# Second layer: where the spectral matrices, the keys' spectra and some element-wise products are computed

## The chip, the cores and the metric

The kernel runs on one core of one Trainium2 chip. Times are microseconds (us) on the device for one execution of the whole program; lower is better. The core has a matrix engine (PE, TensorE; its weight loads are listed as PEld), three engines for element-wise work (DVE or VectorE, ACT or ScalarE, POOL or GpSimd), and queues from which transfers (DMAs) are started; most are started on SP, some on ACT's own queue. Two on-chip memories matter here: SBUF, and PSUM, into which PE writes[...]. A kernel waits for transfers and for other engines by semaphores.

## The reference

Two layers with a residual each, on an image tensor of 4 x 48 x 48 x 128:

```python
    x = x + _L0_conv_ref(_gn(x), ...)
    x = x + _L1_conv_ref(_gn(x), ...)
```

The first is a selective scan in four directions; the change does not touch it. The second takes the image as 4 images of T = 48 channels, each 48 rows (H) by 128 columns (W), and is an attention over the channels whose keys, queries and values are made by spectral convolutions, followed by two more of these:

```python
def _spec_conv(x, w, out_hw):
    xf = jnp.fft.rfft2(x, norm='forward')
    top = jnp.einsum('bimn,iomn->bomn', xf[:, :, :m1, :m2], wc[0])
    bot = jnp.einsum('bimn,iomn->bomn', xf[:, :, -m1:, :m2], wc[1])
    of = of.at[:, :, :m1, :m2].set(top)
    of = of.at[:, :, -m1:, :m2].set(bot)
    return jnp.fft.irfft2(of, s=(Ho, Wo), norm='forward')

def _forward(x, ...):
    xa_n = _inorm(xa, norm_g[0], norm_b[0])
    k = _fno_layer(xa_n, wK, wKs, bKs, (H // 2, W // 2))
    q = _fno_layer(xa_n, wQ, wQs, bQs, (H // 2, W // 2))
    v = _fno_layer(xa_n, wV, wVs, bVs, (H, W))
    scores = jnp.einsum('bhtd,bhsd->bhts', qs, ks) / (np.sqrt(ks.shape[-1]) * TEMPERATURE)
    out = jnp.einsum('bhts,bhsd->bhtd', jax.nn.softmax(scores, axis=-1), vs)
    projd = _fno_layer(out, wP, wPs, bPs, (H, W))
    attention = _inorm(projd + xa, norm_g[1], norm_b[1])
    an = _inorm(attention, norm_g[2], norm_b[2])
    m = _fno_layer(an, wM0, wM0s, bM0s, (H, W), (norm_g[3], norm_b[3]), act=True)
    m = _fno_layer(m, wM1, wM1s, bM1s, (H, W), (norm_g[4], norm_b[4]), act=False)
    return (_inorm(m, norm_g[5], norm_b[5]) + attention).reshape(B, T, H, W)
```

There are 32 heads. `_inorm` normalises each channel's image; `_fno_layer` is a spectral convolution plus a pointwise one. All is float32.

## The kernel before

Layer 0 fills the time up to about 4215 us. Its instructions and those of the last part of layer 1 (the `Strand` class) go through `Ordered`, line 50, which keeps each engine's instructions in the order of the program; that is why so many rows of the profile name L50. The rest of layer 1, in `layer1`, is put in order for each engine by a scheduler, which may move independent instructions past each other; each engine then runs its own list in order.

Layer 1 goes through these stages (times of the profiled execution):

- 4209 to 4258: loads; copies `gblk` and statistics over groups (`bn_stats`), meanwhile the products of the weights of projection and values (`gw`) are transposed and written to DRAM as `dgt`.
- 4258 to 4311: `group_affine` (matmul `gm_l`), the affine map on `xa`, then `first_norm`: means `pm_in`, differences, variances `pv_in`, and the factor `in_r` (line 718). `prepare` loads the weights of keys and queries (`w_wQ`, `w_wK`: many small DMAs on SP, lines 893 to 899) and makes their product `g_qk` by a chain of small DVE instructions.
- 4311 to 4355: `forward_w`, a Fourier transform along the width: PE writes `pa_x`, DVE scales it into `a_x` (two buffers), six DMAs write `da_x` to DRAM, and `load_a2` reads it back turned around as `a2`. Meanwhile PE transposes `xa` into `pxn`, and ACT scales that into `xnt` with the factor `r_t` (from the small matmul `pr`).
- 4356 to 4392: `spectral_weights`, lines 951 to 979. The two MLP convolutions' weights `wM0` and `wM1` (loaded into `w2`) become, for each of 32 frequencies, a 96 x 96 matrix along the height. In 16 rounds of four frequencies POOL makes two products `wih`, PE two matmuls `psw`, ACT copies them into `spw` (one buffer), and a DMA writes that to `sp_d` in DRAM. The matrices are read (as `sp_m`) by the strands, long after.
- 4392 to 4419: `psel` picks the frequencies for queries `qs` and keys `ks` out of `a2`; `pplain` and `ps0` give the scores' part without weights.
- 4419 to 4459: the keys' spectra, in the code the last loop of this block: for each of 16 (image, group of 8 frequencies), two half spectra `pxt` on PE, two ACT copies into `xt` (two buffers), one POOL addition, one DMA to `dxt`. `dxt` is used by the next stage but one.
- 4460 to 4557: the scores. For each of two pairs of images and 12 `jn`, DVE (two of three) or POOL (the third) makes `f`, 128 x 3072, and PE multiplies it with `qs` into four banks `sc`, eight matmuls per `jn`; a last product with `d_qk`; then the softmax, transposes `pat` and copies to `attn_c`.
- 4557 to 4835: the products with the values (`v`, `v3`, `acc`).
- 4835 to 5126: two strands of 96 channels each, by turns: each has phases p0 to p5 with a tail after each (t0 to t5) that is stepped through during the other strand's phase. p1 adds the projection, p2 is the first MLP convolution's part along the height (`pe_m`, `e_m`, with the sums of squares `sqe` into `st_m`, and POOL's `m<-xa,sw`), p3 its part along the width (`pi_m`) with the GELU, p4 and p5 the same for the second convolution and the output. `total` reduces the sums (`red`, `tot_m`), and `product` makes the squares, with frequency 0 halved by the factor `first_k`. In p5, `skip` multiplies eight rows of `m` by `qm` (the tile `sw`) and adds `y` (the image `xa`), and `put` transposes (`pf`), adds a bias (`ot`) and writes the result.

The lines that start the changed parts:

```python
        r0 = first_norm(psst, work, xa)
        prepare()
        ...
        spectral_weights(psum, work)
        ...
            def skip(q):
                for i in range(2):
                    v = self.m[:, 24 * i + q : 24 * i + q + 8]
                    on.gpsimd.tensor_mul(v, v, over(self.qm, 8))
                    on.vector.tensor_add(v, v, self.y[:, 24 * i + q : 24 * i + q + 8])
```

Of the kernel before, what the change touches and what calls it, by code (L numbers as in the profile page):

```python
# [10 lines left out]
F32 = mybir.dt.float32  # L11
BF16 = mybir.dt.bfloat16
AF = mybir.ActivationFunctionType
ALU = mybir.AluOpType
# [15 lines left out]
NH = 32  # L30
# [612 lines left out]
def layer1(ctx, tc, io, x1_dram, out):  # L643
# [5 lines left out]
    nc = tc.nc  # L649
# [298 lines left out]
    def spectral_weights(psum, work):  # L948


        fht = []
        for i, m in enumerate((fh, fhi)):
            p = psum.tile([128, 512], F32, tag="mm", name=f"pfht{i}")
            nc.tensor.transpose(p[0:96, 0:96], m, ident[0:96, 0:96])
            t = work.tile([96, 96], F32, tag=f"fht{i}", name=f"fht{i}", bufs=1)
            nc.scalar.copy(t, p[0:96, 0:96])
            fht.append(t)
        none = work.tile([1, 2, 1], F32, tag="none", name="none", bufs=1)
        nc.gpsimd.memset(none, 0.0)
        for n in range(2):  # L960
            w2 = work.tile([96, 2, 32], F32, tag="w2", name=f"w2_{n}", bufs=2)
            for c in range(2):
                for i in range(2):
                    nc.sync.dma_start(w2[i * 48 : (i + 1) * 48, c], io[f"wM{n}"][c])
            for i in range(2):
                nc.sync.dma_start(w2[48 * i : 48 * i + 1, :, 0:1], none)
            for k0 in range(0, 32, 4):
                p = psum.tile([128, 512], F32, tag="mm", name=f"psw{n}_{k0}")
                for c in range(2):
                    t = work.tile([96, 4, 96], F32, tag="wih", name=f"wih{n}_{k0}_{c}")  # L970
                    nc.gpsimd.tensor_mul(
                        t,
                        ih[:, None].to_broadcast([96, 4, 96]),
                        w2[:, c, k0 : k0 + 4, None].to_broadcast([96, 4, 96]),
                    )
                    nc.tensor.matmul(p[0:96, 0:384], fht[c], t, start=(c == 0), stop=(c == 1))
                t = work.tile([96, 4, 96], F32, tag="spw", name=f"spw{n}_{k0}", bufs=1)
                nc.scalar.copy(t, p[0:96, 0:384].rearrange("p (k m) -> p k m", m=96))
                nc.sync.dma_start(sp_d[n][:, k0 : k0 + 4], t)


    with ExitStack() as ph:
        psum = ph.enter_context(tc.tile_pool(name="l1_ps0", bufs=3, space=PSUM))
        psst = ph.enter_context(tc.tile_pool(name="l1_ps0s", bufs=1, space=PSUM))
        work = ph.enter_context(tc.tile_pool(name="l1_work0", bufs=2))
        mv = small.tile([128, B, 2], F32, tag="mv", name="mv1")
        for b in range(B):
            st = small.tile([128, 6, 6], F32, tag="st", name=f"st1_{b}")
# [29 lines left out]
        for p in range(2):  # L1018
            for q in range(0, H, 4):
# [8 lines left out]
                    AF.Copy,  # L1028
                    scale=r_t[:, p : p + 1],
                )  # L1030
        spectral_weights(psum, work)

        for j in range(4):
            for dst, sel, sel0, one in ((qs, sel_q, sel_q0, one_q), (ks, sel_k, sel_k0, one_k)):
# [37 lines left out]
            nc.tensor.matmul(p[0:T, 0:T], u32[:, bs], u32[:, bs], start=False, stop=True)  # L1072
            nc.scalar.copy(s0[:, b], p[0:T, 0:T])

        for b in range(B):
            for k in range(4):
                xt = work.tile([T, 3, NC], F32, tag="xt", name=f"xt{b}_{k}")
                for e in range(2):
                    p = psum.tile([128, 512], F32, tag="mm", name=f"pxt{b}_{k}_{e}")
                    for i in range(4):  # L1080
                        nc.tensor.matmul(
                            p[0:T, i * 96 : (i + 1) * 96],
                            a2[:, 8 * k + 4 * e + i, b * T : (b + 1) * T],
                            fh,
                            start=True,
                            stop=True,
                        )
                    nc.scalar.copy(
                        xt[:, 0:2].rearrange("t c (k y) -> t k c y", y=48)[:, 4 * e : 4 * e + 4],
                        p[0:T, 0:384].rearrange("t (k c y) -> t k c y", c=2, y=48),  # L1090
                    )
                nc.gpsimd.tensor_add(xt[:, 2], xt[:, 0], xt[:, 1])
                nc.sync.dma_start(dxt[b, k], xt.rearrange("r c n -> r (c n)"))


    with ExitStack() as ph:
        p2 = ph.enter_context(tc.tile_pool(name="l1_p2", bufs=2))
        pf = ph.enter_context(tc.tile_pool(name="l1_pf", bufs=3))
        ps_1 = ph.enter_context(tc.tile_pool(name="l1_ps1", bufs=1, space=PSUM))
        pst = ph.enter_context(tc.tile_pool(name="l1_pst", bufs=2, space=PSUM))  # L1100
        gp = ps_1.tile([128, 3, 4, NH], F32, name="gp_qk")
        nc.scalar.copy(gp, g_qk)
        scale = 2.0 * math.sqrt((H // 2) * (W // 2))
        for pair in range(2):
            sc = ps_1.tile([128, 4, 512], F32, tag="sc", name=f"sc{pair}")
            for jn in range(12):
                j, n = divmod(jn, 3)
                f = pf.tile([128, 2, NH, T], F32, tag="f", name=f"f{pair}_{jn}")
                shape = [128, 2, NH, T]
                on_pool = jn % 3 == 2  # L1110
                (nc.gpsimd if on_pool else nc.vector).tensor_mul(
                    f,
                    (g_qk if on_pool else gp)[:, n, j, None, :, None].to_broadcast(shape),
                    ks[:, j, n, 2 * pair : 2 * pair + 2, None].to_broadcast(shape),
                )
                for g in range(4):
                    for b in range(2):
                        nc.tensor.matmul(
                            sc[64 * b : 64 * b + 64, g, 0 : 8 * T],
                            qs[:, j, n, 2 * pair + b],  # L1120
                            f[:, b, 8 * g : 8 * g + 8],
                            start=(jn == 0),
                            stop=False,
                        )
            for g in range(4):
                for b in range(2):
                    nc.tensor.matmul(
# [6 lines left out]
            for g in range(4):  # L1134
# [18 lines left out]
                for q in range(3):  # L1153
# [4 lines left out]
                    attn_c[:, 2 * pair : 2 * pair + 2, g],  # L1158
                    p[:, 0:384].rearrange("p (q b t) -> p b q t", b=2, t=64),
                )  # L1160
    early.close()


# [144 lines left out]
    eps2 = vec.tile([128, 1], F32, name="eps2")  # L1308
    nc.gpsimd.memset(eps2, 1e-10)
    cst = vec.tile([128, 8], F32, name="cst")  # L1310
    ga, gb, c0, cm, b15, gw0, w11 = (cst[:, i : i + 1] for i in range(7))
    nc.vector.tensor_mul(ga, n_g[:, 1:2], n_g[:, 1:2])
    nc.vector.tensor_scalar(ga, ga, 1e-5, None, ALU.add)
    nc.vector.tensor_mul(gb, n_g[:, 1:2], n_g[:, 2:3])
# [5 lines left out]
    nc.vector.tensor_scalar(cm, cm, -1.0, None, ALU.mult)  # L1320
    nc.vector.tensor_add(b15, n_b[:, 1:2], n_b[:, 5:6])
    nc.vector.tensor_mul(w11, wsm[1], wsm[1])
    a2_all = None

    class Strand:
# [91 lines left out]
        def product(self, e, other, k0, name):  # L1417
# [3 lines left out]
            else:  # L1421
                on.vector.tensor_mul(t, e, other)
            if k0 == 0:
                on.vector.tensor_scalar(t[:, 0], t[:, 0], first_k, None, ALU.mult)
            return [t[:, 4 * i : 4 * i + 4] for i in range(2)]


# [185 lines left out]
        def t4(self):  # L1613
# [10 lines left out]
            on.vector.tensor_mul(v5, t4, v4)  # L1624
            on.vector.tensor_mul(u, t4, cv)
            on.vector.tensor_mul(v5, v5, t4)
            on.vector.tensor_scalar(u, u, wsm[1], 2.0, ALU.mult, ALU.mult)
            on.vector.tensor_add(v5, v5, self.vm)
            on.vector.tensor_add(v5, v5, u)
            s5 = self.rsqrt("s5", v5, eps)  # L1630
# [24 lines left out]
        def p5(self):  # L1655


            def skip(q):
                for i in range(2):
                    v = self.m[:, 24 * i + q : 24 * i + q + 8]  # L1660
                    on.gpsimd.tensor_mul(v, v, over(self.qm, 8))
                    on.vector.tensor_add(v, v, self.y[:, 24 * i + q : 24 * i + q + 8])

            for t in range(6):
# [25 lines left out]
    def over(t, n=QB):  # L1690
        return t[:, None, :].to_broadcast([128, n, P])
# [127 lines left out]
```

## Time and profile before

| | |
|---|---|
| three runs | 5125.19, 5130.29, 5134.14 us; median 5130.29 |
| the profiled execution | 5128.24 us |
| its span | 5126.5 us |
| mean granted PE clock | 0.922 |
| busy in the span: PE, DVE, POOL, ACT | 4220.8, 4231.3, 4054.3, 2907.2 us |
| layer 1 | about 4209 to 5126.5 us |

The profile is of one execution. A row of the timeline or of a group reads: start in us, duration in us (of all its instructions when it ends in xN), engine, line, operation, output<-inputs, shapes, and in square brackets the time for which the engine had been idle before it and what ended that. Part 2 of the page cuts the span into 40 slices of 128 us and gives each engine's busy share in tenths; the last seven to eight slices are layer 1. A sum over a stretch gives, after the stretch and its length, the busy time and number of instructions of PE, PEld, DVE, ACT and POOL, then the granted clock of PE, the share of DMA and its GB/s.

In layer 0 each of DVE and POOL is busy for nearly the whole time; in layer 1 the stages follow each other with different engines busy in each.

### The profile page before, as it was taken

Reading aid. Unit: us, or ns where it says so; the run is one execution under the profiler, and the core shown is the slowest. Engines: PE = TensorE matmul, PEld = TensorE weight load, DVE = VectorE, ACT = ScalarE, POOL = GpSimd, SP = SyncE. Lnnn points to the kernel's source line nnn. Section 1 sums busy time; section 2 is a strip of 40 time slices with the busy share of each in tenths; the row PEclk is TensorE's granted clock in tenths of the full one; section 3 lists DMA queues with packets and bytes.
Section 4 is the critical chain, followed back from the end, with each engine's and each line's share of the span. In section 5 each row is a group of like instructions: output and inputs, shape, how many; then the busy total and the mean of one; then the engine's idle time right before and its main releaser. Section 6 shows DMA issues by size and latency. Waiting matters only on the chain. (4 is left out here: it accounts for less than half of the span.)

```text
span 5126.5 us, 44328 instructions
## 1 busy us (share of the span) xinstructions
PE 4220.8 (82%) x12344; PEld 1901.0 (37%) x12344; DVE 4231.3 (83%) x2887; ACT 2907.2 (57%) x6438; POOL 4054.3 (79%) x2223
## 2 busy tenths in 40 slices
PE   6889898878898988888989888878787866888876
PEld 3334333333343333333433333333333323443343
DVE  3689998989899989899999898999999964166545
ACT  3666666666565676666666766666565633213343
POOL 3589998989899988898999888899999860446433
PEclk8999999999999999999999999999999887889877
DMA  1223232323333322232333232333333226136536
GB/s 53 76 84 104 95 113 91 102 86 100 94 107 102 106 90 98 87 102 93 105 106 102 92 99 88 105 99 106 98 101 97 90 67 139 47 83 183 152 90 142
DMA packets 276767, 509.25 MB, mean 99 GB/s; under 512 B 100602, under 2 KB 185434, under 8 KB 276326
## 3 DMA queue, kind: packets, MB, share of 16 engines
q1 hardware_dynamic: 265846, 502.66, 32.1%
q10 hardware_dynamic: 10672, 3.76, 0.4%
q8 instruction: 97, 1.59, 0.1%
q14 instruction: 152, 1.25, 0.1%
HBM read 462.58 MB, written 43.72 MB: 99 GB/s over the span
## 5 line engine op out<-in xcount | busy, mean ns | idle before, releaser
L50 POOL TENSOR_TENSOR hc<-h,cbc 128x960 f32<-128x960 f32 (+1 forms) x1280 | 2716.5, 2137 | 464.7 <-DVE h L50 336.1
L50 DVE TENSOR_TENSOR_SCAN h<-da,carry,db 128x961 f32<-128x961 f32 (+1 forms) x1280 | 2701.0, 2129 | 122.1 <-ACT carry L50 87.8
L50 ACT ACTIVATE da<-dt,a_neg 128x480 f32<-128x480 f32 (+1 forms) x2560 | 1661.3, 649 | 1251.3 <-DVE h L50 1206.3
L50 PE MATMUL yp<-hc,ident 128*128 128x480 f32 (+1 forms) x5120 | 2276.5, 572 | 7.1 <-POOL hc L50 6.9
L50 PEld LDWEIGHTS yp<-hc,ident 128*128 128x128 f32 x5120 | 1007.8, 199 | 1421.9 <-issue 1011.1
L50 DVE TENSOR_TENSOR db<-du,pb 128x960 f32<-128x960 f32 (+1 forms) x960 | 1062.3, 1107 | 210.2 <-PE pb L50 154.6
L50 PE MATMUL pb<-bs,pick 112*128 112x480 bf16 (+1 forms) x960 | 361.6, 377 | 399.1 <-DVE db L50 397.2
L50 POOL TENSOR_TENSOR db<-du,bbc 128x960 f32<-128x960 f32 (+1 forms) x320 | 687.9, 2150 | 0.0
L50 PE MATMUL pc<-pad,cdiag 128*128 128x480 f32 (+1 forms) x630 | 283.3, 561 | 10.7 <-ACT pad L50 10.7
L1236 POOL TENSOR_TENSOR v<-grep,xrep 128x768 f32<-128x768 f32 x96 | 173.7, 1820 | 107.3 <-PE acc L1240 52.2
L50 POOL TENSOR_TENSOR du<-dt,xc 128x480 f32<-128x480 f32 (+1 forms) x160 | 204.3, 1277 | 37.7 <-ACT dt L50 37.7
L50 PE MATMUL px<-xc,w_xp 128*112 128x480 f32 (+1 forms) x320 | 216.2, 763 | 16.9 <-ACT xc L50 13.3
L1240 PE MATMUL acc<-v,attn_c 128*64 128x384 f32 x1152 | 211.7, 505 | 22.2 <-POOL v L1236 17.2
L50 ACT COPY db<-carry 128x1 f32<-128x1 f32 x1280 | 226.0, 177 | 7.0 <-DVE db L50 3.7
L1232 DVE TENSOR_TENSOR v<-gp,xrep 128x1536 f32<-128x1536 f32 x96 | 164.5, 1753 | 78.5 <-DMA xrep<-dxt 36.2
L50 PEld LDWEIGHTS <-pick 112*128 112x128 bf16 x960 | 97.9, 102 | 333.9 <-issue 310.3
L50 PE MATMUL pd<-xd,w_dt 8*128 8x480 f32 (+1 forms) x320 | 168.6, 607 | 39.8 <-ACT bs L50 25.5
L50 ACT ACT_TABLE_LOAD x146 | 187.3, 1283 | 23.4 <-PE gv_g L50 13.7
L50 ACT COPY carry<-h 128x2 f32<-128x2 f32 x1024 | 192.6, 188 | 0.0
L50 PEld LDWEIGHTS pc<-pad,cdiag 128*128 128x128 f32 x630 | 122.1, 195 | 144.2 <-issue 114.9
L50 PE MATMUL yp<-y,ident 128*128 128x480 f32 (+1 forms) x240 | 166.2, 822 | 0.2
L1240 PEld LDWEIGHTS acc<-v,attn_c 128*64 128x64 f32 x1152 | 90.3, 140 | 139.9 <-issue 52.6
(366 smaller groups left out, 3192.0 us busy)
## 6 DMA issues: line engine op xcount, KB each, us to landing
cbc<-cd SPq DMA_DIRECT2D x512, 480.0 KB
bbc<-cd SPq DMA_DIRECT2D x256, 240.0 KB
cbc<-cd SPq DMA_DIRECT2D x128, 384.0 KB
xrep<-dxt SPq DMA_DIRECT2D x384, 72.0 KB
grep<-dgt SPq DMA_DIRECT2D x32, 576.0 KB
bbc<-cd SPq DMA_DIRECT2D x64, 192.0 KB
dgt<-gtt SPq DMA_DIRECT2D x4, 2304.0 KB
x<-in_xT SPq DMA_DIRECT2D x16, 288.0 KB
```

What stands on the lines that cost most here:

```text
L50: return lambda *args, **kw: self._tc.keep_in_program_order(emit(*args, **kw))
L1232: nc.vector.tensor_mul(v, gp[:, None, :, 0:NC].to_broadcast([128, 2, 2, NC]), x[:, :, 0:2])
L1236: nc.gpsimd.tensor_mul(v3, r[:, 2:3].to_broadcast([128, 2, NC]), x[:, :, 2])
L1240: nc.tensor.matmul(acc[c][64 * b : 64 * b + 64, 0:NC], attn_c[:, 2 * pair + b, g, q], v[:, b, c] if c < 2 else v3[:, b], start=first, stop ...
```

## The change

Four parts, all in layer 1.

1. `spectral_weights` is called before the statistics, at the start of its block, instead of after the transposes. Its loads of `wM` (12 small DMAs) go to ACT's queue instead of SP's.
2. The keys' spectra become a generator, `keys`, whose halves are issued between the score products, one or two after each `jn`. `xt` has one buffer instead of two, and its products have one PSUM bank. `f` is made in two halves, one for each image of the pair, in five buffers of half the size instead of three.
3. The factor `first_k` of `product` and the factor `wsm[1] * 2` of t4 are applied by ACT (`self.times`, an activation with a scale) instead of DVE; the second one's value is made ahead, as `w2`.
4. `skip` multiplies on DVE instead of POOL.

```diff
@@ spectral_weights
-                    nc.sync.dma_start(w2[i * 48 : (i + 1) * 48, c], io[f"wM{n}"][c])
+                    nc.scalar.dma_start(w2[i * 48 : (i + 1) * 48, c], io[f"wM{n}"][c])
             for i in range(2):
-                nc.sync.dma_start(w2[48 * i : 48 * i + 1, :, 0:1], none)
+                nc.scalar.dma_start(w2[48 * i : 48 * i + 1, :, 0:1], none)
@@ layer1
         work = ph.enter_context(tc.tile_pool(name="l1_work0", bufs=2))
+        spectral_weights(psum, work)
         mv = small.tile([128, B, 2], F32, tag="mv", name="mv1")
...
-        spectral_weights(psum, work)
...
-        for b in range(B):
-            for k in range(4):
-                xt = work.tile([T, 3, NC], F32, tag="xt", name=f"xt{b}_{k}")
...
-        pf = ph.enter_context(tc.tile_pool(name="l1_pf", bufs=3))
+        pf = ph.enter_context(tc.tile_pool(name="l1_pf", bufs=5))
...
+        psx = ph.enter_context(tc.tile_pool(name="l1_psx", bufs=1, space=PSUM))
+        def keys():
+            for b in range(B):
+                for k in range(4):
+                    xt = p2.tile([T, 3, NC], F32, tag="xt", name=f"xt{b}_{k}", bufs=1)
+                    for e in range(2):
+                        p = psx.tile([128, 512], F32, tag="xt", name=f"pxt{b}_{k}_{e}")
+                        for i in range(4):
+                            nc.tensor.matmul(
+                                p[0:T, i * 96 : (i + 1) * 96],
+                                a2[:, 8 * k + 4 * e + i, b * T : (b + 1) * T],
+                                fh,
+                                start=True,
+                                stop=True,
+                            )
+                        nc.scalar.copy(
+                            xt[:, 0:2].rearrange("t c (k y) -> t k c y", y=48)[:, 4 * e : 4 * e + 4],
+                            p[0:T, 0:384].rearrange("t (k c y) -> t k c y", c=2, y=48),
+                        )
+                        yield
+                    nc.gpsimd.tensor_add(xt[:, 2], xt[:, 0], xt[:, 1])
+                    nc.sync.dma_start(dxt[b, k], xt.rearrange("r c n -> r (c n)"))
+        beside = keys()
...
-                f = pf.tile([128, 2, NH, T], F32, tag="f", name=f"f{pair}_{jn}")
-                shape = [128, 2, NH, T]
+                shape = [128, NH, T]
                 on_pool = jn % 3 == 2
-                (nc.gpsimd if on_pool else nc.vector).tensor_mul(
-                    f,
-                    (g_qk if on_pool else gp)[:, n, j, None, :, None].to_broadcast(shape),
-                    ks[:, j, n, 2 * pair : 2 * pair + 2, None].to_broadcast(shape),
-                )
+                f = []
+                for b in range(2):
+                    f.append(pf.tile(shape, F32, tag="f", name=f"f{pair}_{jn}_{b}"))
+                    (nc.gpsimd if on_pool else nc.vector).tensor_mul(
+                        f[b],
+                        (g_qk if on_pool else gp)[:, n, j, :, None].to_broadcast(shape),
+                        ks[:, j, n, 2 * pair + b, None].to_broadcast(shape),
+                    )
...
-                            f[:, b, 8 * g : 8 * g + 8],
+                            f[b][:, 8 * g : 8 * g + 8],
...
+                for _ in range(2 - jn % 2 if pair == 0 else 1 + jn % 2):
+                    next(beside, None)
...
+        for _ in beside:
+            pass
@@ layer1, constants
+    nc.vector.tensor_scalar(w2, wsm[1], 2.0, None, ALU.mult)
@@ Strand.product
             if k0 == 0:
-                on.vector.tensor_scalar(t[:, 0], t[:, 0], first_k, None, ALU.mult)
+                self.times(t[:, 0], t[:, 0], first_k)
@@ Strand.t4
-            on.vector.tensor_scalar(u, u, wsm[1], 2.0, ALU.mult, ALU.mult)
+            self.times(u, u, w2)
@@ Strand.p5, skip
-                    on.gpsimd.tensor_mul(v, v, over(self.qm, 8))
+                    on.vector.tensor_mul(v, v, over(self.qm, 8))
```

## The prediction

> **What bounds the kernel now.** I read the page first, then the timeline of the second layer (4209 to 5126 us of a span of 5126.5), then sums over stretches, then single tiles. The page's part 2 shows where there is anything to win: in the last eight of the 40 slices DVE and POOL fall from nine tenths to between one and six, while PE stays at seven or eight.
>
> ```profile
> PE   6889898878898988888989888878787866888876
> DVE  3689998989899989899999898999999964166545
> POOL 3589998989899988898999888899999860446433
> ```
>
> The part of the page on the chain that ended last names only 14 pieces from 5114.89 us on, so the order of stages must be read from the timeline. The sums over stretches show two stages (us, then busy time of PE, PEld, DVE, ACT, POOL) in which DVE does nothing: 4357 to 4392 makes spectral weights, 4419 to 4460 the keys' spectra.
>
> ```profile
> 4357.00:4392.00 35.00, 30.02 (x64) 9.78 (x64) 0.00 (x0) 6.53 (x16) 24.21 (x30) 0.85 0.19 55
> 4419.00:4460.00 41.00, 29.14 (x256) 26.89 (x255) 0.00 (x0) 14.57 (x34) 15.79 (x16) 0.79 0.39 87
> ```
>
> In the timeline the first one's pace is a DMA: each copy into `spw`, which has one buffer, waits for the transfer out of it. The second ends in a wait of DVE for the last transfer of a key spectrum; the line above it is the work the keys are now put beside, where PE is held by `f`.
>
> ```profile
> 4364.87 0.47 ACT L978 COPY spw<-psw 96x384 f32<-96x384 f32 x1 [1.99 <-DMA sp_d<-spw]
> ...
> 4431.62 1.52 PE L1081 MATMUL pxt<-fh,a_x 96*48 96x96 f32 x16 [0.15 <-ACT xt L1088]
> ...
> 4460.43 6.62 DVE L1111 TENSOR_TENSOR f<-gp_qk,ks 128x3072 f32<-128x3072 f32 x2 [45.33 <-DMA dxt<-xt]
> ...
> 4478.72 7.96 PE L1118 MATMUL sc<-f,qs 128*64 128x384 f32 x48 [0.41 <-POOL f L1111]
> ```
>
> Later a single multiplication of 96x96 numbers holds DVE for 26.14 us, while POOL runs 24 products without a gap; PE waits 23.84 us behind it.
>
> ```profile
> 4932.95 26.14 DVE L50 TENSOR_SCALAR sqe<-sqe,first_k 96x96 f32<-96x96 f32 x1 [6.42 <-ACT sqe L50]
> ...
> 4937.81 21.21 POOL L50 TENSOR_TENSOR xa<-xa,s 128x768 f32<-128x768 f32 x12
> 4959.01 0.54 DVE L50 TENSOR_REDUCE red<-st_m 128x96 f32<-128x384 f32 x1
> 4959.61 0.50 PEld L50 LDWEIGHTS tot_m<-red,g 128*128 128x128 f32 x2 [24.08 <-DVE red L50]
> 4959.61 0.74 PE L50 MATMUL tot_m<-red,g 128*128 128x96 f32 x2 [23.84 <-DVE red L50]
> ```
>
> And in the last stage DVE waits for POOL's products.
>
> ```profile
> 5068.92 12.77 POOL L50 TENSOR_TENSOR m<-m,sw 128x768 f32<-128x768 f32 x6
> 5070.75 5.01 DVE L50 TENSOR_TENSOR m<-m,xa 128x768 f32<-128x768 f32 x2 [10.21 <-POOL m L50]
> ```
>
> **What the Trainium skill says.** "SBUF — State Buffer", section "Who interferes with whom": a DVE instruction with two SBUF inputs, or one in a two-port performance mode, shares a port pair with a GpSimd instruction reading SBUF; the lock is held for the whole instruction; PE and ACT never wait for it. The trace agrees: `first_k` took 266 ns at best and 26142 ns at worst, and `e_m<-e_m,t` 0.95 us alone, 2.47 beside POOL. That one instruction is passed over by some fourteen POOL instructions is in the trace, not in the page. "DMA: Bandwidth & Descriptors" gives a fixed cost of about 2 us per DMA; the trace has 1.99 us of wait per `spw`.
>
> **Spectral matrices ahead.** What it would remove: `a_x` is back at 4355.5, and `psel` starts at 4392.44, so 36.9 us are spent on these matrices. But the order of PE's instructions in the new program has only two transposes and four of the 16 `psw` before the statistics; the other twelve come behind `pr`, ahead of `pa_x`, which begins the forward transform. ACT has one `spw` early, 15 behind `r_t`. With one buffer each costs 0.47 us of copy and 1.98 of wait, 2.44 in the trace. So:
> - the four early `psw` took 8.5 us (4357.1 to 4365.5) in before; `gm_l`, at 4258.7, then starts about 5 later (2 to 7: part lies in the time in which DVE stands until 4248.5);
> - 12 loads of `wM` now lie on ACT's queue in the tail of layer 0: mostly in ACT's gaps, +1 (0 to 6);
> - `in_r` came at 4311.3; the 15 copies take 15 x 2.44 = 36.6, less the PSUM buffers that let PE go ahead (3 buffers): `pa_x` can begin near 4342 and the first `a_x` be done at 4350 where it was 4313.4; the g_qk chain of DVE is behind the same loads of `w_wK` on SP, which stand between the `sp_d` transfers. The last `da_x` leaves near 4365 (was 4336.29); `pu` came 19.2 after it: `psel` at 4385.5, with the 6 from above 4391.5, against 4392.44.
> Then `psel` to `ps0` without the transfers is about 1.5 shorter. I take -1 in all for this part: the work has moved past the transform, not beside it. Bounds: -36 if `pa_x` isn't held, +12 if the delays ahead are the upper ones.
>
> **Keys between the products.** Removed: the stage from 4418.9 to 4460.3. The first `f` can start at 4417.4 + (-1 + 1) of the part above, 42.9 earlier. Added: PE gets 32 halves of 0.76 (1.52 for two), 24.3 us. The products before: `d_qk` of the first pair ends 40.6 after the first `f`, of the second 86.4; a period of 8.36 for three jn, of which 7.96 is PE. PE is thus nearly full, and the 24.3 us lie on the path, save what fits its waits (0.41 a period, and the two starts). `xt` and its PSUM bank have one buffer: a round of two halves, two copies of 0.47, one add of 0.99 behind POOL's `f` halves (2.67 each) and a transfer of about 2.2 comes to some 6 us. Following the instructions by hand I get 48.6 for the first pair and 102.2 for the second: +15.8. One more for the last `dxt`, which now stands ahead of the loads for the next stage on SP. Five half-size buffers of `f` for three whole ones change nothing: half h takes the place of h-5, near enough double buffering. -42.9 + 15.8 + 1 = -26; with the 1 above I write -25 here and -1 there (bounds -34, PE's waits taking half of it, to -12, a round of 7).
>
> **Small factors off DVE.** `first_k` on ACT costs about 0.37 (row `s<-s,n_g`; here 96x96). The 26.14 goes. `red` then starts at 4934.3, `tot_m` near 4936; `e_m` is loaded from 4936.72 on and lands near 4945; from `red` to `pi_m` the trace has 9.74 (4959.01 to 4968.75), which gives 4944; `t<-t,s` and `e_m<-e_m,t` have two SBUF inputs and POOL runs until 4959, so 2 more, as in the pairs 0.95 and 2.47. `pi_m` at 4946 against 4968.75: -22 (0 to -25). What is late next is the landing of `e_m`, one us before. The other three `first_k` and `u` on ACT: nothing, they're 0.3 to 1.7 us beside PE's work. The chain behind it (p3, p4, p5) has no other input that is later, so the gain lasts.
>
> **Last products on DVE.** POOL's six cost 12.77 and 13.57 per strand (2.13 to 2.26 each), and in strand 0 they stand behind the `xr` additions, until 5067.16, though `sw` was there at 5055.7. On DVE a round of q is `e_m` 0.95, two products and two sums of 0.93, four of 0.50: 6.7, three times 20. Strand 0's p5 ran from 5059.6 to 5094 with p4's end beside it; the 10.21 of wait goes, DVE's contended sums (5.01 and 3.42 for two, alone 1.82) too, and 5.6 of products come: -5 to -10. Strand 1: 5097.35 to 5120.65 is 23.3; 20 now: -3.5. If the cover, PE's `pf` and ACT's `ot`, isn't as short as DVE, nothing below 5097 + 18 is possible. Together -12 (-8 to -15).
>
> Sum: -1 - 25 - 22 - 12 = -60. The profiled execution took 5128.24, 1.7 over its span, and lies 2 below the median 5130.29: 5068 as a profile, 5070 as a median.
>
> **Rivals.**
> A: the matrices do get hidden, because `pa_x` overtakes or the copies don't wait in that place (their transfers overlap idle queues). For: DVE and POOL are idle there. Against: PE's order is fixed, and one buffer. 5070 - 34 = 5036.
> B: the stall moves to the next DVE instruction with two SBUF inputs (`t<-t,s`, until POOL ends at 4959.02). For: the same queue of POOL's 24. Against: DVE's tensor_tensor instructions get in by turns elsewhere (13.27 for four beside POOL at 4286.90). Then the 22 are lost: 5092.
> C, the slower side: the single `xt` buffer holds PE, which stands in order: each `pxt` waits for a transfer that waits for an add behind two `f` halves. The worst round is 1.5 + 0.9 + 5.3 + 1 + 2.2 = 10.9; 16 of these are 174 where I have 102. It ends the gain from (102 + 60)/16 = 10.1 and makes it measurably slower from 10.8; at 11.2, 5070 + (179 - 102) = 5147. Against: POOL has an `f` at only every third jn.
> D: the delays ahead of the statistics and a round of 7 both come in: +12 + 13, 5095.
>
> **How the numbers follow.** Forecast 0.5, A 0.2, B 0.15, D 0.1, C 0.05. Likeliest: 5070, its own range 5052 to 5086. The range reaches to A and to B and D: 5030 to 5106; outside is C and a joint B and D. A measurement of this kernel can tell about 0.2%, 10 us. Faster than 5120: all but C and a rest of D: 0.92; within 0.03; slower 0.05.
>
> **What would show it.** In the new profile: a `spw` row with some 2 us of DMA wait still, but between `r_t` and `pa_x`, and the first `da_x` near 4350; the first `f` near 4417 and the second pair's `d_qk` some 102 after; no DVE instruction over 6 us after 4900 and `pi_m` about 10 behind `red`; `m<-m,sw` on DVE at 0.93. I'd be wrong if `psel` starts below 4375 (A), if a small DVE instruction of 10 us or more stands there (B), or if `pxt` waits 4 us and more for `xt` (C).

## The result and the profile after

The changed kernel took 5085.36 us (median of five runs, 5073.73 to 5089.75) against 5130.29 before (median of five, 5115.78 to 5134.14): a ratio of 0.9918, with a 95% interval of 0.9899 to 0.9937. It is faster by 0.8%, where 1.2% (5070) was predicted. The profiled execution has a span of 5083.1 us, 43.4 less than before.

The busy shares by slice, for the lines shown of the kernel before:

```profile
PE   6889898888798988887989888878787785888876
DVE  3689998989899989898999898999999983356536
POOL 4589998988899989798999898899999872346531
```

Counted from 1, slice 35 of DVE, which held the idle stages, has filled from 1 to 3: the scores have moved forward into it. In the last slice DVE went from 5 to 6 and POOL from 3 to 1, the products of the last stage. The rest is read best by taking the same events in both timelines, each counted from the start of the load of `xa` (4219.7 before, 4218.1 after; 1.6 us of the gain lie in layer 0, which is the same in both, and over all traces this start lies between 4215.7 and 4221.8). Every event is given by the start of its instruction.

| event, us after the load of xa | before | after | change of the stage that ends here | predicted |
|---|---|---|---|---|
| first `psel` | 172.7 | 172.7 | 0.0 | -1 |
| first `f` | 240.7 | 193.7 | -47.0 | -43 |
| last product with `d_qk` | 326.5 | 300.7 | +21.2 | +16 |
| first `acc` | 355.1 | 329.6 | +0.3 | +1 |
| last `acc` | 611.5 | 590.4 | +4.4 | 0 |
| first `red` of `st_m` | 739.3 | 693.5 | -24.7 | -25 |
| first `pi_m` of p3 | 749.0 | 719.7 | +16.5 | +3 |
| first `ot` | 857.8 | 817.8 | -10.7 | -8 |
| last `ot` | 902.3 | 860.8 | -1.5 | -4 |

The first row says that up to `psel` nothing was gained by moving the matrices; the second and third say that the keys' stage is gone and that the scores pay nearly half of it. All this was in the sum, though not in these sizes. The row of `pi_m` was not: of the 24.7 us won up to `red`, 16.5 are lost again within the next 26. The timeline of the changed kernel shows where:

```profile
4911.57 0.56 DVE L50 TENSOR_REDUCE red<-st_m 128x96 f32<-128x384 f32 x1 [8.35 <-PE st_m L50]
...
4915.37 21.20 POOL L50 TENSOR_TENSOR xa<-xa,s 128x768 f32<-128x768 f32 x12
4915.56 0.75 DVE L50 RECIPROCAL t<-t 128x96 f32<-128x96 f32 x1 [1.81 <-ACT t L50]
...
4916.35 20.35 DVE L50 TENSOR_TENSOR t<-t,s 128x96 f32<-128x96 f32 x1
...
4936.73 0.96 DVE L50 TENSOR_TENSOR e_m<-e_m,t 128x768 f32<-128x768 f32 x1
4937.79 3.02 PE L50 MATMUL pi_m<-e_m,iw 64*128 64x384 f32 x8 [15.86 <-issue]
```

`red` runs at 4911.57, as it should with the 26.14 us gone. But the next DVE instruction with two operands in SBUF, `t<-t,s` with 96 elements a row, is recorded with 20.35 us, and it ends when POOL's twelve products end (4936.57). `RECIPROCAL`, just before it and with one operand, took its usual 0.75 beside the first of these products. The stall has not gone; it has found another instruction.

### The profile page after: what moved, and what is told of

It is laid out like the page before. It is cut to its first block, busy times and chain, and to the rows that moved or that the text cites. A ratio compares the mean times of both kernels' runs of the same rounds, so it can differ in the third digit from the quotient of the medians.

```text
span 5083.1 us, 44364 instructions
## 1 busy us (share of the span) xinstructions
PE 4214.9 (83%) x12344; PEld 1897.5 (37%) x12344; DVE 4225.4 (83%) x2908; ACT 2911.3 (57%) x6446; POOL 4033.8 (79%) x2219
## 5 line engine op out<-in xcount | busy, mean ns | idle before, releaser
L1252 PE MATMUL acc<-v,attn_c 128*64 128x384 f32 x1152 | 212.8, 511 | 25.8 <-POOL v L1248 15.8
```

Of the source, the lines that this page charges most:

```text
L1252: nc.tensor.matmul(acc[c][64 * b : 64 * b + 64, 0:NC], attn_c[:, 2 * pair + b, g, q], v[:, b, c] if c < 2 else v3[:, b], start=first, stop ...
```

## The experiments

Runs of one kernel differ: eleven of the kernel before, beside the ninth to eleventh experiment, lie between 5108.34 and 5140.23. So the experiments are read by intervals between events in their traces, and by the time of the program only where there were several runs. The stage of `acc`, which no experiment touches, took from 253.4 to 267.0 us over all traces: the 4.4 in the table is within what this stage varies by itself.

**First: `first_k` on ACT and nothing else**, in the kernel before.

```diff
-                on.vector.tensor_scalar(t[:, 0], t[:, 0], first_k, None, ALU.mult)
+                self.times(t[:, 0], t[:, 0], first_k)
```

> The kernel before with one edit: first_k is applied by ACT. Theory 1 (the obstacle is POOL's unbroken queue of 24 products; any DVE instruction with two SBUF inputs that comes while it runs is passed over until its end): the 26.14 us goes, but t<-t,s then stands until POOL ends near 4959, and pi_m comes about 8 us earlier than in the kernel before (near 4960), the whole 5120. Theory 2 (only the in-place scaling by first_k is passed over): pi_m 22 us earlier, near 4946, the whole 5106.

It took 5127.47 in one run (5120 was expected), 5135.03 the kernel before beside it.

```profile
4947.75 0.56 DVE L50 TENSOR_REDUCE red<-st_m 128x96 f32<-128x384 f32 x1 [7.86 <-PE st_m L50]
...
4951.43 21.22 POOL L50 TENSOR_TENSOR xa<-xa,s 128x768 f32<-128x768 f32 x12
...
4952.52 20.24 DVE L50 TENSOR_TENSOR t<-t,s 128x96 f32<-128x96 f32 x1
...
4973.85 3.05 PE L50 MATMUL pi_m<-e_m,iw 64*128 64x384 f32 x8 [15.75 <-issue]
```

`t<-t,s` stands for 20.24. Here the way to POOL's row was longer than in the other two traces (its first product lies 87 us behind the first `pe_p`, not 80; PE's granted clock over this stretch was 0.74, and 0.82 in the kernel before), so the start of POOL's 24 products is the fair zero: `pi_m` follows it by 52.2 in the kernel before (4916.60 to 4968.75), by 43.7 in the changed kernel (4894.11 to 4937.79) and by 43.7 here (4930.2 to 4973.85). Counted so, the edit is worth 8.4 us, as theory 1 said, and this is what used to follow the end of POOL's queue: 9.74 us from `red` to `pi_m` before, where now 1.2 lie between the end of the queue (4972.65) and `pi_m`.

**Second: POOL's products held back.**

```diff
-            self.times(self.s1, self.s1, n_g[:, 1:2])
...
+                if t == 0:
+                    self.times(self.s1, self.s1, n_g[:, 1:2])
                 r = 8 * (3 * (t % 2) + t // 2)
```

The first line is in t1, the others in p3, behind the GELU.

> The changed kernel, with s1 scaled by n_g on ACT behind the first GELU of p3 instead of in t1, so that POOL's products xa<-xa,s can't start before the first pi_m. Theory 1 (POOL's queue is the obstacle): t<-t,s takes 0.3 us, pi_m follows red by about 12 us, limited by the load of e_m, instead of 26; the whole 13 us less, 5072. Theory 2 (t<-t,s is held by something else, or the delayed POOL products hold p4 instead): pi_m stays, or the gain is given back later; 5085.

```profile
4907.97 0.56 DVE L50 TENSOR_REDUCE red<-st_m 128x96 f32<-128x384 f32 x1 [8.19 <-PE st_m L50]
...
4912.74 0.26 DVE L50 TENSOR_TENSOR t<-t,s 128x96 f32<-128x96 f32 x1
4914.85 0.96 DVE L50 TENSOR_TENSOR e_m<-e_m,t 128x768 f32<-128x768 f32 x1 [1.85 <-DMA e_m<-de_m]
...
4918.25 2.93 PE L50 MATMUL pi_m<-e_m,iw 64*128 64x384 f32 x8
```

`t<-t,s` takes 0.26, `e_m<-e_m,t` waits for its transfer only, and `pi_m` follows `red` by 10.3 us (26.2 in the changed kernel). Of these 15.9 us, 4.2 are lost later (from `pi_m` to the last `ot` 145.3 instead of 141.1; that POOL is now later with the image is the likely cause, but was not tested). The run took 5069.58. Theory 1 holds: without POOL's products at this place the small product isn't held.

**Third: `t` through PSUM**, so that `t<-t,s` has one operand in SBUF, and POOL's queue stays.

```diff
-            self.t3 = self.rsqrt("t3", self.s22, eps)
-            on.vector.tensor_mul(self.t3, self.t3, self.s2)
+            self.t3 = self.vector("t3")
+            on.scalar.activation(self.spare, self.s22, AF.Sqrt, bias=eps)
+            on.vector.reciprocal(self.spare, self.spare)
+            on.vector.tensor_mul(self.t3, self.spare, self.s2)
```

`self.spare` is a free part of the PSUM bank of `tot_m`.

> The changed kernel, with the square root and reciprocal before t<-t,s written to PSUM, so that t<-t,s has one SBUF input only. POOL's queue is untouched. Theory 1a (every DVE instruction with two SBUF inputs waits for the end of the queue): e_m<-e_m,t, 128x768, then stands for 20 us, pi_m as in the changed kernel, 5085. Theory 1b (a long DVE instruction gets in by turns with POOL, as in the last stage, and only short ones are passed over): t<-t,s 0.3 us, e_m<-e_m,t about 2.5, pi_m about 12 to 14 behind red, 5073. Where t<-t,s stands for 20 us still, the port is not what holds it.

```profile
4903.26 21.22 POOL L50 TENSOR_TENSOR xa<-xa,s 128x768 f32<-128x768 f32 x12
...
4904.34 0.26 DVE L50 TENSOR_TENSOR t<-tot_m,s 128x96 f32<-128x96 f32 x1
4906.39 18.90 DVE L50 TENSOR_TENSOR e_m<-e_m,t 128x768 f32<-128x768 f32 x1 [1.80 <-DMA e_m<-de_m]
4925.36 0.63 PEld L50 LDWEIGHTS pi_m<-e_m,iw 64*128 64x128 f32 x4 [15.67 <-issue]
4925.39 3.03 PE L50 MATMUL pi_m<-e_m,iw 64*128 64x384 f32 x8 [15.46 <-issue]
```

Theory 1a: with one operand in PSUM the same small product runs in 0.26 beside POOL, and the stall moves on by one instruction, to one with eight times as many elements. So among these instructions it isn't the size that tells which one is held, but the two operands in SBUF. That such an instruction is not always held is shown further down. The whole took 5070.26 in one run, but its stage of `acc` was the shortest of all, 253.4; from `red` to `pi_m` it has 25.8, nothing won.

**Fourth: the matrices back at their old place.** `spectral_weights` is called behind the transposes again; the loads stay on ACT's queue.

```diff
-        spectral_weights(psum, work)
         mv = small.tile([128, B, 2], F32, tag="mv", name="mv1")
...
+        spectral_weights(psum, work)
```

> The changed kernel with spectral_weights at its old place behind the transposes (its loads still on ACT's queue); all other parts of the change kept. By the prediction's account the matrices only moved past the forward transform: psel starts at the same time after the start of layer 1 (within 3 us), the whole 5085. Rival (the move hid them): psel about 35 us later, the whole 5120.

```profile
4403.84 0.48 ACT L978 COPY spw<-psw 96x384 f32<-96x384 f32 x1
4404.37 0.44 PEld L1041 LDWEIGHTS psel<-a_x,sel 96*32 96x32 f32 x2 [0.17 <-ACT spw L978]
...
4426.93 6.75 DVE L1119 TENSOR_TENSOR f<-gp_qk,ks 128x1536 f32<-128x1536 f32 x4 [4.68 <-PE pxt L1091]
```

`psel` comes 177.8 us after the load of `xa`, 5.1 later than in the changed kernel and more than the account's 3. It is also 5.1 later than before the change: halves of `pxt`, free to move now, stand ahead of the matrices with `pu` and wait for `a_x` too. From `psel` to the first `f` it takes 27.6 us, and 21.0 in the changed kernel: the last copies of `spw` lie among PE's `psel` here, as in the kernel before, and hold some of it. So the first `f` comes 11.6 us later (205.3 against 193.7), and the start of `acc` too (341.2 against 329.6). Between these two traces, with the other parts in place, moving the matrices is thus worth 11.6 us, more than half of it behind `psel`; the rival's 35 are far off. The time was 5095.73 in one run. The span is 10.8 longer than in the changed kernel's trace: 11.6 are this, 3.5 lie in layer 0 and 2.3 in a slower `acc` (263.1 against 260.8), and 6.6 are won back behind `acc`, where the two kernels are the same.

**Fifth: two buffers of `xt`**, and four halves of `f` to make room for them.

```diff
-                    xt = p2.tile([T, 3, NC], F32, tag="xt", name=f"xt{b}_{k}", bufs=1)
+                    xt = p2.tile([T, 3, NC], F32, tag="xt", name=f"xt{b}_{k}", bufs=2)
-        pf = ph.enter_context(tc.tile_pool(name="l1_pf", bufs=5))
+        pf = ph.enter_context(tc.tile_pool(name="l1_pf", bufs=4))
```

> The changed kernel with two buffers of xt, and four half buffers of f instead of five to make room. From the first f to the last product with d_qk the changed kernel took 107.0 us, of which PE was busy for 98.8 and waited 8.5 for xt. Theory 1 (PE's own work is the bound): the wait falls to 2 or 3 at most, the stretch to 101 to 103, no more. Theory 2 (the single xt paces the whole phase, the prediction's round of 6 us): the stretch falls to near 91, what PE had without the keys plus a little. Were four buffers of f too few, it would rise.

The stretch rose to 117.5 us, the case named last. The waits over it (who waited for what: us, times, longest), first of the changed kernel and then of this one:

```profile
ACT xt L1098 <- DMA dxt<-xt: 36.0, 9, 5.6
...
PE pxt L1091 <- ACT xt L1098: 8.5, 7, 2.5
...
PEld sc L1126 <- POOL f L1119: 0.4, 1, 0.4
```

```profile
PEld sc L1126 <- POOL f L1119: 17.0, 10, 3.3
...
PE sc L1126 <- POOL f L1119: 12.3, 8, 2.7
...
PE pxt L1091 <- ACT xt L1098: 4.8, 6, 1.7
```

ACT's wait for the transfer out of `xt`, 36.0 before, isn't among the waits any more, and PE's wait for `xt` fell from 8.5 to 4.8; but PE now waits 12.3 us for POOL's `f`. So two changes met: for PE the single `xt` costs about the 8.5 that it waits, and the fifth half of `f` is worth more than that. What a second `xt` alone gives wasn't measured, for there is no room for it beside five halves.

**Sixth: the last products back on POOL.**

```diff
-                    on.vector.tensor_mul(v, v, over(self.qm, 8))
+                    on.gpsimd.tensor_mul(v, v, over(self.qm, 8))
```

> The changed kernel with the products m*qm of the last stage on POOL again. By the prediction: 12 us more from the first pi_m to the last ot (141.1 in the changed kernel, 153.3 before), most of it before the first ot. Rival (the gain there came from the other parts, since POOL now finishes xr earlier): no difference over 3 us.

From the first `pi_m` to the last `ot` it has 151.1 us, 10.0 more than the changed kernel, 7.6 of it before the first `ot`. The part is worth 10 of the 12 us that were foretold.

**Seventh: POOL's products on a scratch tile without gaps.** The image is then not scaled by `s1`, so the residual at the end is another one.

```diff
                 r = 8 * (3 * (t % 2) + t // 2)
-                v = self.y[:, r : r + 8]
+                v = self.flat
                 on.gpsimd.tensor_mul(v, v, over(self.s1, 8))
```

> The changed kernel, with POOL's 12 products xa<-xa,s of p3 made on a scratch tile with the same number of elements that lies without gaps in SBUF (the image is left unscaled by s1, so the residual is another one): number, place and length of POOL's products stay. It asks why DVE gets in by turns beside m<-m,sw (2.5 us for an addition) but not beside xa<-xa,s. Theory P (the pattern of POOL's operands: one of m<-m,sw runs without gaps, both of xa<-xa,s are in rows of 96): t<-t,s takes at most 2.5 us, and pi_m follows red by 14 instead of 26. Theory Q (nothing in the products; an unbroken queue passes over DVE whatever they read): t<-t,s stands for about 20 us again.

```profile
4914.63 24.45 POOL L50 TENSOR_TENSOR flat<-flat,s 128x768 f32<-128x768 f32 x12
...
4915.46 1.14 DVE L50 TENSOR_TENSOR t<-t,s 128x96 f32<-128x96 f32 x1
4917.57 1.62 DVE L50 TENSOR_TENSOR e_m<-e_m,t 128x768 f32<-128x768 f32 x1 [0.97 <-DMA e_m<-de_m]
...
4920.97 2.93 PE L50 MATMUL pi_m<-e_m,iw 64*128 64x384 f32 x8
```

DVE is let in here, at the end of one product each time, and POOL's twelve take 24.45 instead of 21.2. Theory P foretold this. The time was 5068.64 in one run. But the edit changed two things: all products on one tile also wait for each other, and the trace has 0.07 us between two of them, where the products on the image overlap by 0.04. And it is one trace. The tenth to the twelfth show what that is worth.

**Eighth and ninth: the matrices split.** Four rounds ahead of the statistics, twelve one by one between the transposes; three buffers of `spw`. In the ninth, their transfers go on ACT's queue.

```diff
-                t = work.tile([96, 4, 96], F32, tag="spw", name=f"spw{n}_{k0}", bufs=1)
+                t = work.tile([96, 4, 96], F32, tag="spw", name=f"spw{n}_{k0}", bufs=3)
...
-                nc.sync.dma_start(sp_d[n][:, k0 : k0 + 4], t)
+                nc.scalar.dma_start(sp_d[n][:, k0 : k0 + 4], t)
+                yield
...
-        spectral_weights(psum, work)
+        matrices = spectral_weights(psum, work)
+        for _ in range(4):
+            next(matrices)
...
                     scale=r_t[:, p : p + 1],
                 )
+                next(matrices, None)
```

The eighth has `nc.sync` still.

> The changed kernel with the spectral matrices split: four of 16 rounds ahead of the statistics, twelve put one by one between the transposes behind the forward transform, and three buffers of spw. In the changed kernel psel starts 172.7 us after the load of xa, as in the kernel before (172.7). If the matrices can be hidden in the wait for the return of a_x, psel comes about 18 us earlier, at 155, and the whole at 5067; if they can't (ACT's copies hold the transposes, or SP's transfers the return), within 5 us of 172.7.

It missed: `psel` at 174.0, the whole 5095.41. SP's queue in its timeline says why:

```profile
4319.77 0.33 SPq L979 DMA_DIRECT2D sp_d<-spw  x1
...
4320.14 2.04 SPq L893 DMA_DIRECT2D w_wK<-in_wK  x6
...
4323.25 4.40 SPq L899 DMA_DIRECT2D w_wK<-in_wK  x15
...
4340.79 0.29 SPq L733 DMA_DIRECT2D da_x<-a_x  x1
```

The fourth early transfer stands on SP until ACT has copied its `spw`, at 4319.27, behind `r_t`; the loads of `w_wK` are behind it, and the first `da_x` behind these, 119.1 us after the load of `xa` instead of 98.1 before the change, though the first `a_x` was done at 97.5. (In the changed kernel it is 135.2, but there `a_x` itself is done only at 130.2.)

> The split matrices with their transfers on ACT's queue instead of SP's. Theory S (in the first split SP, which takes its transfers in order, stood from the third spw on until ACT came to it behind r_t, and held the loads of w_wK and behind them da_x): the first da_x leaves 100 us after the load of xa or earlier, as before (98), and psel comes at 147 to 155 instead of 174. Otherwise, if ACT's queue holds the return of a_x now, psel at 165 or later.

The first `da_x` now leaves at 104.1, but `psel` comes at 165.8, not at 147 to 155: theory S is right as to SP, and something else takes more than half of the gain. The other branch, 165 or later, fits the number; its reason, that ACT's queue holds the return of `a_x`, was not tested. `in_r` is there 10 us later than before the change (100.8 against 91.3), and ACT waits 16.2 us in two places for a transfer out of `spw`. 5069.59 in one run.

**Tenth: `s1` written out eight times**, so that one operand of POOL's product has no gaps.

```diff
-            self.times(self.s1, self.s1, n_g[:, 1:2])
+            self.s1_8 = self.blk("xr", [128, 8, P], "s1_8", 2)
+            self.times(self.s1_8, over(self.s1, 8), n_g[:, 1:2])
...
-                on.gpsimd.tensor_mul(v, v, over(self.s1, 8))
+                on.gpsimd.tensor_mul(v, v, self.s1_8)
```

> The changed kernel with s1 written out eight times by ACT into a scratch tile without gaps (one copy of about 0.85 us per strand), so that of the two operands of POOL's xa<-xa,s only the image is read in rows of 96. Theory P, in its narrow form (POOL gives way when one operand lies without gaps, as in xa<-xa,xr and m<-m,sw): t<-t,s at most 2.5 us, pi_m about 10 to 14 behind red, the whole near 5070. If both operands must lie without gaps but for a repeated one, as in the scratch-tile run: t<-t,s stands for about 20 us, 5085.

**Eleventh: this and the ninth together.**

> The changed kernel with both: matrices split and on ACT's queue, and s1 written out for POOL. By the two theories above the gains add, 18 to 24 and 12 to 15: 5050 (5044 to 5058). If one of them is off the path once the other is in, 5065 to 5072.

It took 5077.15 (median of six), far from the 5050 foretold. The same two lines of the tenth's timeline and then of the eleventh's:

```profile
4914.29 23.45 POOL L50 TENSOR_TENSOR xa<-xa,s 128x768 f32<-128x768 f32 x12
...
4915.78 0.43 DVE L50 TENSOR_TENSOR t<-t,s 128x96 f32<-128x96 f32 x1
```

```profile
4910.53 21.21 POOL L50 TENSOR_TENSOR xa<-xa,s 128x768 f32<-128x768 f32 x12
...
4911.90 19.95 DVE L50 TENSOR_TENSOR t<-t,s 128x96 f32<-128x96 f32 x1
```

The same instructions on POOL and on DVE, and `t<-t,s` begins 1.49 us and 1.37 us behind the first product: once DVE is let in at the end of that product, once it is passed over at eleven ends. The times would fit this: the tenth's four runs are 5066.31 (the one with this trace) and then 5079.33, 5083.76 and 5084.77; the eleventh's six are 5063.39 and five from 5075.58 to 5081.35 (the trace is that of 5077.53). But only one run of each has a trace, and the spread of the kernel before in the same rounds is larger, so that two groups of times are not shown. By medians they are 5081.55 and 5077.15, with ratios of 0.9905 (0.9879 to 0.9931) and 0.9899 (0.9876 to 0.9922) to the kernel before: no clear gain over the changed kernel, whose own five runs are four from 5084.95 to 5089.75 and one of 5073.73. The narrow form of theory P has fallen: with the same pattern DVE was let in once and passed over once. Whether the scratch tile of the seventh would always let DVE in isn't known.

**Twelfth: nothing left to chance.** POOL's products held back as in the second, the matrices as in the ninth with two early rounds instead of four.

> The changed kernel with POOL's products held back behind the first GELU, as in the second experiment, and the split matrices on ACT's queue with two rounds instead of four ahead of the statistics. If it is chance whether DVE is let in between POOL's products, this kernel has nothing left to be let in for at that place: t<-t,s 0.3 us, pi_m about 10 behind red in the profile, and its runs have no second group some 14 us higher, as those of the kernel with s1 written out had. psel at 156 to 160 after the load of xa (172.7 in the changed kernel), the whole 5060 (5052 to 5067). If the four early rounds were not what delayed in_r by 10 us, psel stays at 166 and the whole is 5066.

5057.93 (median of four, 5054.00 to 5062.47); the kernel before beside it 5129.08; ratio 0.9857, interval 0.9838 to 0.9877. `pi_m` follows `red` by 10.3 us, and none of the four runs lies some 14 us above the others. `psel` comes at 161.5, `in_r` at 93.6 instead of 100.8: the early rounds had delayed it. What keeps `psel` from 156 is in the timeline, where ACT, whose copies now alternate with the transposes' scaling, waits for one transfer out of `spw` while `a_x` is being read back:

```profile
4347.21 1.57 PE L976 MATMUL psw<-wih,fht 96*96 96x384 f32 x4
...
4355.12 0.47 ACT L978 COPY spw<-psw 96x384 f32<-96x384 f32 x1 [8.25 <-DMA sp_d<-spw]
...
4355.65 1.09 PE L1026 MATMUL pxn<-ident,xa 128*96 128x128 f32 x4 [6.87 <-ACT spw L978]
```

PE stood for 6.87 of this. The kernel beats the one before by 71 us. It was not run beside the changed kernel; the medians differ by 27 us, and the intervals of the two ratios (0.9899 to 0.9937 for the changed one) lie apart.

Its trace also says what is left of theory P. POOL's products stand later here, unaltered and in rows of six, and a DVE instruction with two operands in SBUF meets them:

```profile
4943.71 11.41 POOL L50 TENSOR_TENSOR xa<-xa,s 128x768 f32<-128x768 f32 x6 [16.68 <-ACT s L50]
...
4949.52 2.17 DVE L50 TENSOR_TENSOR e_m<-e_m,t 128x768 f32<-128x768 f32 x1
```

`e_m<-e_m,t` ends at 4951.69, at the end of one product and 3.4 us before the row's end; the second experiment's trace has the same at 4960.98 (2.06 us). Beside products of this very pattern `e_m<-e_m,t` stood for 18.90 us in the third experiment, and the products overlap by 0.05 us here. So the pattern does not decide, and DVE needs no gap between the products to get in. In the kernel before, even one and the same row did both: `first_k` was let in near its beginning, 13.5 us before it was held for 26.14.

```profile
4916.60 19.54 POOL L50 TENSOR_TENSOR m<-xa,sw 128x768 f32<-128x768 f32 x11 [79.44 <-ACT sw L50]
...
4919.42 0.82 DVE L50 TENSOR_SCALAR sqe<-sqe,first_k 96x96 f32<-96x96 f32 x1 [3.37 <-issue]
```

## Why the prediction was right or wrong

Right in direction and within its range; 15 us too fast in its number, and most of it in one step, the third below.

- *Spectral matrices ahead: -1.* Measured 0.0 at `psel`, and more behind it (next point). The mechanism was as the prediction read it from the order: the 15 `spw` behind `r_t` have 26.9 us of waits, nearly all for their transfers, and hold `pa_x`, whose first `a_x` comes 129.7 after the load of `xa` (91.6 before). `gm_l` came 5.0 later in this count, as estimated. Rival A fell: by its sign `psel` would have started below 4375, and it started at 4390.8.
- *Keys between the products: -25.* Measured -25.8 from `psel` to the last `d_qk`. That this is so near is luck, for its two terms are off in opposite directions. The first `f` came 4 us earlier than worked out, since `psel` to `ps0` shrank by 6.4 us (22.2 to 15.8) without the copies of the matrices among it, not by 1.5. So part of what the fourth experiment gives to the moved matrices is booked here. And the scores got 21.2 longer, not 15.8. In the sums over the two halves of the scores in the changed kernel PE is busy for 98.8 of 107.2 us (75.0 of 86.3 before, plus the 24.3 that the prediction gave to the keys is 99.3):

```profile
4411.80:4462.60 50.80, 47.58 (x336) 27.37 (x336) 34.30 (x21) 8.64 (x17) 32.53 (x17) 1.00 0.14 31
4462.60:4519.00 56.40, 51.26 (x340) 28.96 (x340) 29.54 (x32) 11.14 (x24) 26.55 (x15) 0.94 0.19 49
```

   PE stood for 11.3 us before and for 8.4 after. The keys' work did fill the old waits: PE waits for `f` hardly at all now. But of the 8.4 nearly everything is new, the wait for the single `xt` (8.5 in the list of waits under the fifth experiment). Without it the scores would have been longer by some 13 us, an estimate from 24.3 - 11.3. So the wait that rival C named was there, and the count by hand didn't have it at this size. Rival C's own size, 5147, was far off, and its sign did not come: no single wait was longer than 2.5. "Five half-size buffers of f change nothing" is unproved; four cost more than a second `xt` gave.
- *Small factors off DVE: -22.* This is the step that failed. Measured -8.2 from the first `pe_p` behind `acc` to `pi_m` (-24.7 up to `red`, +16.5 behind it). The text gave the contended `t<-t,s` and `e_m<-e_m,t` "2 more, as in the pairs 0.95 and 2.47"; it was 20.35. It took DVE's turn beside POOL from places where it came after one product, and not from the place concerned, where the very trace showed fourteen passed over. Rival B was this mechanism, held at 0.15, and it mispriced it in the other direction ("then the 22 are lost"): what used to follow the end of POOL's queue, from `red` to `pi_m`, now comes before it, and that is the 8. The sign that the prediction gave for B came: a small DVE instruction of over 10 us behind 4900, and `pi_m` 26 behind `red` instead of 10.
- *Last products on DVE: -12.* Measured -12.2 from `pi_m` to the last `ot`, and 10.0 when undone. The wait of strand 0 went as said: from its first `e_m` of p5 to its last sum it took 23.5 us instead of 31.1, where 5 to 10 were foretold. What stayed is that DVE's sums now meet POOL's `xr` additions (2.38 for one instead of 0.95). Strand 1, from its first `e_m` of p5 to the last `ot`, took 21.0 instead of 24.7; 3.5 were foretold. (The table's -1.5 counts from the first `ot` of strand 0.)

The sum with the measured terms: -1.6 (layer 0) + 0.0 - 25.8 + 0.3 + 4.4 - 8.2 - 12.2 - 0.3 (behind the last `ot`) = -43.4.

In its first reading of the page the prediction gives PE seven or eight tenths and DVE and POOL one to six in the last eight slices; the lines have six to eight for PE and a zero for POOL. Nothing in the sum rests on this.

Of the Trainium skill's statements, that of "SBUF — State Buffer", section "Who interferes with whom", carried further than it was trusted: a DVE instruction with two SBUF inputs stood, one with a PSUM input or with one input did not (0.26 and 0.75 beside products of the same kind). The 2 us from "DMA: Bandwidth & Descriptors" stand there in the section "Anatomy of one DMA — SWDGE (gpsimd) path", as a fit to transfers issued from GpSimd; those of `spw` start on SP, and in the changed kernel twelve of ACT's waits for them were 1.97 to 2.06 us, one 2.99.

## What to carry to other kernels

When a wait is taken away from one instruction, ask whether its cause is still there for the next: here it was POOL's unbroken row of 24 products, and moving the row (2 lines) gave what moving the victim did not. Work moved ahead in the text can hold what then comes behind it: read PE's, ACT's and SP's order, since here one store that waited on SP held the loads behind it, and the stores of `a_x` behind these. Judge such a move by the first instruction behind the whole stage: in the fourth experiment it was worth 5.1 us at `psel` and 11.6 at the first `f`. And a trace is one execution: the same instructions at the same place showed 0.43 us in one kernel's trace and 19.95 in another's.

## What the runs showed of the hardware

A DVE instruction with two operands in SBUF, or one that scales in place by a factor in SBUF, can be passed over by a whole row of POOL instructions. It happened in ten traces, each time until the end of the row: 26.14 us for `first_k` in the kernel before, 18.90 for `e_m<-e_m,t`, and 19.95 to 20.41 for `t<-t,s` in the other eight. All nine traces in which POOL's row at this place was unaltered show it. It is not the rule for every row, nor for every instruction in one row. Near the beginning of that row and beside `m<-m,sw` in the kernel before, on the scratch tile, in one of two traces with `s1` written out, and beside the rows of six in the second and the twelfth, DVE got in at the end of the product under way; after the longer of such DVE instructions (0.95 us alone) POOL's next product took about 2.5 us instead of 1.80. What decides it was not found: not the size of DVE's instruction, not the pattern of POOL's operands, not a gap between its products.
